# A GRU with a mixture of experts behind it: gates in three stages, and up projections without transposes of act

## The chip, the cores and the metric

The kernel runs on one core of a Trainium2 chip. The metric is the device time of one execution in microseconds (us). Beside it stand the profile of one execution and its trace, taken by the hardware profiler. The engines are named as in the profile: PE is TensorE (PEld its weight loads), DVE is VectorE, ACT is ScalarE, POOL is GpSimd, SP is SyncE.

## The reference, cut to what matters

`x` has 8 sequences of 256 steps with 512 features. A GRU runs over the steps, and its states go through a feed-forward block with one shared expert of 1024 inner features and eight routed experts of 256, two for each token. All is float32.

```
for each step:
    gi = x_t @ W_ih + b_ih                  # 512 -> 3 * 512
    gh = h @ W_hh + b_hh
    r = sigmoid(i_r + h_r);  z = sigmoid(i_z + h_z)
    n = tanh(i_n + r * h_n)
    h = (1 - z) * n + z * h
probs = softmax(h @ w_gate);  two experts per token, weights renormalised
routed = sum over the two: weight * ((silu(g) * u) @ w_down[e]),   g, u = split(h @ w_gate_up[e])
shared = (silu(g) * u) @ w_sh_down,                                g, u = split(h @ w_sh_gate_up)
out = x + routed + shared
```

## The kernel before, in words

**Recurrence.** `step(n)` (L348) is one of 256 steps. The batch is only 8, so the weights of a matmul are 8 columns of the transposed state `hT`, and W_hh is the moving operand. The 512 outputs of a gate are split into four column groups `j` that use four parts of TensorE's columns side by side, each writing its own 32 partitions of PSUM. Gates r and z share the tile `ps_rz` (256 columns), n has `ps_n` (128). ScalarE puts the seeds of the next step into PSUM ahead of the matmuls (`open_gates`, L337): the input part of r and z, and the bias of n. After the matmuls VectorE transposes `ps_rz` (L364) and `ps_n` (L370) in blocks of 32, ScalarE takes the sigmoid of r and z together (L366) and the tanh (L375), and VectorE makes the new state from `omz` = 1 - z, `zh` = z * h and `nn` (L379 to L383). GpSimd copies the state into `hc`, which collects the 16 states of a block of 128 tokens (L386).

A float32 matmul shows as two records in the trace, each with a weight load. A matmul in column groups is four such pairs, one for each group.

**Filler.** While the gates are being computed, TensorE works off a queue of pieces: the input projections of coming blocks (`project`, L282; tile `gip`), and the shared expert for the block of 16 steps that is complete. `MM` = 0.86 is the planner's cost of a piece, and pieces can be halved. After each step the main loop (L778) issues so many pieces that the queue of the block is spread evenly over the steps that are left. The instructions of an engine run in the order in which they are issued, so a step's matmuls stand behind the filler that was issued before them.

**Shared expert.** It is cut into four units of 256 inner features (`shared_unit`, L630, through `unit`, L570). A unit has four up pieces (one for each quarter `q` of the 512 features): the tokens are the weights, in four groups of 32 columns (`multiply`, L255), and 512 columns of `wsu` move past; tile `gu_s`. Then comes `gated` (L564): a sigmoid on ScalarE and two products on VectorE give `act`, with tokens on the partitions. `turn` (L586) transposes `act` with two 128x128 matmuls into `actTp_s`, and ScalarE copies that to `actT_s`. Two down pieces (tile `po`) then use `actT_s` as weights. `feed` (L709) interleaves the units: the first half of a unit's up pieces, the turn of the unit two feeds back, the second half, then the downs. A block's last unit is turned and finished in the next block.

**Other users of TensorE.** The transposes of `x` (`xTp`) and of `hc` (`hrp`, `send_rows` L486), and the router (`choose` L394, tile `lgp`; `order_experts`, `weigh`, `give_places`). PSUM has one buffer for `ps_rz`, one for `ps_n`, three for `ps_mm`, two for transposes (`ps_t`) and one for `po`.

**After the last step** `by_groups` is false: `multiply` then issues full 128-column matmuls. The last block's shared units run with the routing work between them (L806). Then 39 tiles of 128 token-expert pairs (`tile_unit`, L653) run: rows fetched by an indirect DMA on GpSimd's queue, transposed (`xrTp`), up (`gu_t`), turned (`actTp_t`), down (`yp`), and added into the output by an indirect DMA.

## Time and profile before

| | |
|---|---|
| device time, three runs | 1550.34, 1552.07, 1553.2 us; median 1552.07 us |
| the profiled execution | 1548.32 us, of which the span from first to last instruction is 1546.5 us |
| granted TensorE clock, mean of the span | 0.992 |
| busy | PE 1487.6, PEld 778.0, DVE 688.4, ACT 359.6, POOL 210.5 us |
| recurrent matmuls | ps_rz 8192 records, mean 380 ns; ps_n 8192 records, mean 273 ns |
| shared experts' up, gu_s | 257.0 us busy; records of 512 columns mean 594 ns, of 256 columns 380 ns |
| transposes of act in the shared experts, actTp_s | 128 records, 27.7 us busy, mean 298 ns |
| their copies on ScalarE, actT_s | 64, 23.5 us busy, mean 368 ns |
| seeds on ScalarE | ps_rz 256 copies, mean 369 ns; ps_n 256 copies, mean 259 ns |

How to read it: a row of a group gives the line, engine, operation, tiles and shapes, then busy time and the mean of one, then the idle time of the engine ahead of such instructions and what ended it. In `128*8 128x256` the part before the space is the weights (rows * columns), the part after it what moves past. Records of matmuls overlap: [...] In the timeline, a line begins with the start and the length in us of a merged group of instructions.

### The profile page before, as it was taken

Reading aid. Unit: us, or ns where it says so; the run is one execution under the profiler, and the core shown is the slowest. Engines: PE = TensorE matmul, PEld = TensorE weight load, DVE = VectorE, ACT = ScalarE, POOL = GpSimd, SP = SyncE. Lnnn points to the kernel's source line nnn. Section 1 sums busy time; section 2 is a strip of 40 time slices with the busy share of each in tenths; the row PEclk is TensorE's granted clock in tenths of the full one; section 3 lists DMA queues with packets and bytes.
Section 4 is the critical chain, followed back from the end, with each engine's and each line's share of the span. In section 5 each row is a group of like instructions: output and inputs, shape, how many; then the busy total and the mean of one; then the engine's idle time right before and its main releaser. Section 6 shows DMA issues by size and latency. Waiting matters only on the chain.

```text
span 1546.5 us, 53864 instructions
## 1 busy us (share of the span) xinstructions
PE 1487.6 (96%) x22969; PEld 778.0 (50%) x22969; DVE 688.4 (45%) x2747; ACT 359.6 (23%) x1351; POOL 210.5 (14%) x419
## 2 busy tenths in 40 slices
PE   4999999999999999999999999999999999999997
PEld 1455555555555555555555555555555544444443
DVE  2445454545454445454545454545454542222222
ACT  0222222222222222222222222222222221222221
POOL 2001110101000001010101010101010102444443
PEclk8999999999999999999999999999999999999998
DMA  7613130303020202010201010101010314445454
GB/s 256 201 40 108 14 87 13 100 13 101 13 60 13 60 13 59 14 52 15 57 16 50 17 41 18 48 18 48 18 53 13 84 49 135 75 89 96 84 93 62
DMA packets 59055, 92.70 MB, mean 60 GB/s; under 512 B 8960, under 2 KB 29504, under 8 KB 58816
## 3 DMA queue, kind: packets, MB, share of 16 engines
q1 hardware_dynamic: 48056, 66.89, 14.8%
q0 software_dynamic: 10624, 22.10, 7.7%
q8 instruction: 182, 2.98, 0.8%
q14 instruction: 57, 0.47, 0.1%
q10 hardware_dynamic: 136, 0.26, 0.1%
HBM read 57.85 MB, written 31.37 MB: 58 GB/s over the span
## 4 chain that ended last, share of the span: by engine, by line
PE 91%; DVE 4%; issue 2%; ACT 1%; DMA 1%; DVEq 0%; SPq 0%; POOLq 0%; POOL 0%; ACTq 0%
PE ps_rz L355 29%; PE ps_n L355 15%; PE gu_s L260 12%; PE gip L260 10%; PE gu_t L574 9%; PE po L260 6%; PE yp L679 4%; PE actTp_s L589 1%; DVE gn L370 1%; PE xrTp L660 1%; PE lgp L398 1%; ACT nn L375 1%; DMA x<-in_x_dram 1%; DVE nt L372 1%; DVE nt L373 1%
## 5 line engine op out<-in xcount | busy, mean ns | idle before, releaser
L355 PE MATMUL ps_rz<-we,hT 128*8 128x256 f32 x8192 | 491.2, 380 | 21.4 <-DVE hT L383 10.8
L355 PEld LDWEIGHTS ps_rz<-we,hT 128*8 128x8 f32 x8192 | 223.2, 89 | 298.8 <-ACT ps_n L343 56.3
L364 DVE STREAM_TRANSPOSE gT<-ps_rz 128x256 f32<-128x256 f32 x256 | 115.2, 450 | 397.2 <-PE ps_rz L355 397.1
L355 PE MATMUL ps_n<-we,hT 128*8 128x128 f32 x8192 | 271.9, 273 | 0.0
L260 PE MATMUL gu_s<-wsu,hc 128*32 128x512 f32 (+2 forms) x2376 | 257.0, 518 | 0.0
L355 PEld LDWEIGHTS ps_n<-we,hT 128*8 128x8 f32 x8192 | 225.9, 90 | 53.2 <-issue 0.5
L366 ACT ACTIVATE rz<-gT 128x64 f32<-128x64 f32 x256 | 65.6, 256 | 710.1 <-DVE gT L364 710.1
L386 POOL COPY hc<-hT 128x32 f32<-128x32 f32 x256 | 62.3, 243 | 1111.4 <-DVE hT L383 1111.4
L260 PE MATMUL gip<-we,xT 128*32 128x512 f32 (+1 forms) x1952 | 189.7, 510 | 2.1 <-ACT xT L247 2.1
L574 PE MATMUL gu_t<-we,xrT 128*128 x312 | 146.7, 593 | 0.2 <-ACT xrT L662 0.2
L260 PE MATMUL po<-wsd,actT_s 128*32 128x512 f32 (+2 forms) x1132 | 131.2, 532 | 13.3 <-ACT actT_s L591 13.3
L370 DVE STREAM_TRANSPOSE gn<-ps_n 128x128 f32<-128x128 f32 x256 | 81.1, 317 | 122.5 <-PE ps_n L355 115.2
L260 PEld LDWEIGHTS gu_s<-wsu,hc 128*32 128x32 f32 (+1 forms) x2376 | 77.2, 111 | 89.2 <-issue 79.4
L375 ACT ACTIVATE nn<-nt 128x32 f32<-128x32 f32 x256 | 58.7, 229 | 185.1 <-DVE nt L373 185.1
L341 ACT COPY ps_rz<-seeds 128x256 f32<-128x256 f32 x256 | 94.5, 369 | 22.0 <-DMA seeds<-gid_rz 21.5
L260 PEld LDWEIGHTS gip<-we,xT 128*32 128x32 f32 x1952 | 58.0, 110 | 72.2 <-issue 60.9
L567 DVE TENSOR_TENSOR act_t<-gu_t,act_t 128x256 f32<-128x256 f32 x39 | 16.6, 424 | 146.3 <-ACT act_t L566 146.3
L685 POOL DMA_INDIRECT out_dram<-y,row x39 | 61.6, 1579 | 124.7 <-DVE y L682 95.8
L679 PE MATMUL yp<-we,actT_t 128*128 x156 | 73.4, 593 | 0.5 <-ACT actT_t L591 0.5
L574 PEld LDWEIGHTS gu_t<-we,xrT 128*128 128x128 f32 x312 | 53.3, 190 | 38.7 <-issue 38.0
L260 PEld LDWEIGHTS po<-wsd,actT_s 128*32 128x32 f32 (+1 forms) x1132 | 38.0, 112 | 57.8 <-issue 33.5
L343 ACT COPY ps_n<-seed_hn 128x128 f32<-128x128 f32 x256 | 66.4, 259 | 0.0
(139 smaller groups left out, 974.1 us busy)
## 6 DMA issues: line engine op xcount, KB each, us to landing
gid_rz<-gi SPq DMA_DIRECT2D x16, 512.0 KB
seeds<-gid_rz SPq DMA_DIRECT2D x256, 32.0 KB
we<-in_L_ffn_w_gate_up_dram SPq DMA_DIRECT2D x8, 1024.0 KB
gid_n<-gi SPq DMA_DIRECT2D x16, 256.0 KB
seeds_n<-gid_n SPq DMA_DIRECT2D x256, 16.0 KB
wsu<-_L_ffn_w_sh_gate_up_dram SPq DMA_DIRECT2D x8, 512.0 KB
rows<-hr SPq DMA_DIRECT2D x16, 256.0 KB
again<-in_x_dram SPq DMA_DIRECT2D x16, 256.0 KB
```

Of the source, the lines that this page charges most:

```text
L260: nc.tensor.matmul(ps[rows_], lhs[:, rows_], rhs, start=start, stop=stop, skip_group_check=True)
L341: nc.scalar.copy(ps_rz, seeds[c % NS][:, t, 0 : 2 * P])
L343: nc.scalar.copy(ps_n, seed_hn)
L355: nc.tensor.matmul(ps[32 * j : 32 * j + B, :].rearrange("p (a i) -> p a i", i=32), hT[:, q, 0:B], whh_v[:, q, lo:hi, j, :], start=False, s ...
L364: nc.vector.transpose(gT.rearrange("p a b -> p (a b)"), ps_rz)
L366: nc.scalar.activation(rz, gT[:, :, 0:B], AF.Sigmoid)
L370: nc.vector.transpose(gn.rearrange("p a b -> p (a b)"), ps_n)
L375: nc.scalar.activation(nn, nt, AF.Tanh)
L386: nc.gpsimd.tensor_copy(hc_of[k].rearrange("p q (b t) -> p q b t", t=TS)[:, :, :, t], new)
L574: multiply(box["ps"][:, cols], lhs(q), w_up(q)[:, cols], start=(q == 0 and cols.start == 0), stop=(q == NQ - 1 and cols.stop == D),)
L679: nc.tensor.matmul(box["y"], lhs, rhs, start=(f == 0), stop=(f == NF - 1))
L685: nc.gpsimd.indirect_dma_start(out=out.rearrange("b t d -> (b t) d"), out_offset=bass.IndirectOffsetOnAxis(ap=laid["row"][:, i : i + 1], a ...
```

## The change

The diff, cut to its core:

```diff
-    ps_t = ctx.enter_context(tc.tile_pool(name="ps_t", bufs=2, space=PSUM))
+    ps_t = ctx.enter_context(tc.tile_pool(name="ps_t", bufs=1, space=PSUM))
...
+    banks = {g: ps_gru.tile([P, D], F32, name=f"ps_{g}") for g in "rnz"}
...
+    def for_transposes(shape, name):
+        if by_groups[0]:
+            return ps_t.tile([P, *shape], F32, tag="tp", name=name)
+        spare.rotate(-1)
...
     def step(n):
...
+        for g, bank in banks.items():
+            lo = "rzn".index(g) * NQ
             for q in range(NQ):
                 for j in range(4):
                     nc.tensor.matmul(
-                        ps[32 * j : 32 * j + B, :].rearrange("p (a i) -> p a i", i=32),
+                        bank[32 * j : 32 * j + B, 0:P].rearrange("p (a i) -> p a i", i=32),
                         hT[:, q, 0:B],
-                        whh_v[:, q, lo:hi, j, :],
+                        whh_v[:, q, lo : lo + NQ, j, :],
...
+        gr = turned("r")
+        r = made("r")
+        nc.scalar.activation(r, gr, AF.Sigmoid)
+        open_gate(n + 1, "r")
+        gn = turned("n")
+        nt = made("nt")
+        nc.vector.tensor_tensor(nt, gn, r, ALU.mult)
+        open_gate(n + 1, "n")
         nc.vector.tensor_tensor(nt, nT_of[c][:, ts, :, 0:B], nt, ALU.add)
+        nn = made("nn")
         nc.scalar.activation(nn, nt, AF.Tanh)
+        gz = turned("z")
+        z = made("z")
+        nc.scalar.activation(z, gz, AF.Sigmoid)
+        open_gate(n + 1, "z")
+        hn = made("hn")
+        nc.vector.tensor_tensor(hn, hT[:, :, 0:B], nn, ALU.subtract)
+        nc.vector.tensor_tensor(hn, z, hn, ALU.mult)
+        nc.vector.tensor_tensor(new, nn, hn, ALU.add)
...
     def shared_unit(k, c, n):
...
+            for q in qs:
+                for g in range(4):
+                    fs = slice(f * P + 32 * g, f * P + 32 * g + 32)
+                    nc.tensor.matmul(
+                        box["ps"][32 * g : 32 * g + 32, m, :],
+                        wsu[c][:, q, two_i, fs],
+                        hc_of[k][:, q, :],
...
+                    lambda cols, f=f: into(f, cols, box["act"][:, f, :], wsd[c][:, f, cols])
...
+    def feed_at_once(stages):
+        assert not stages[0] and under_way["up"] is None
+        under_way["up"] = stages
+        feed(None)
...
+    spare.extend(banks.values())
```

The gates get a PSUM bank each, `ps_r`, `ps_n` and `ps_z`, and TensorE computes them in this order. Each has its own seed copy, its own 32-block transpose on VectorE and its own activation. The new state is n + z * (h - n).

In a shared unit the roles of the operands are swapped for the up projections. 32 columns of `wsu` are the weights of each column group, the 128 tokens of `hc` move past, and `gu_s` and `act` have inner features on the partitions. One up piece is one of the four blocks of 128 inner features over all `q`. The down pieces use `act` as weights, and the unit has no turn. The up matmuls stay in column groups after the last step too. `feed_at_once` queues a unit's ups and then the downs of the unit before it; a block's last downs still go into the next block, behind its first unit's ups.

`ps_t` has one buffer. After the last step transposes take the three gate banks in turn. Expert tiles are computed as before.

More of the change, by code (lines that the diff above doesn't have):

```diff
@@ L229 @@
     nc.gpsimd.dma_start(listed[E * NM : E * NM + 1], vacant[0:1])
-    ps_rz = ps_gru.tile([P, 2 * P], F32, name="ps_rz")
-    ps_n = ps_gru.tile([P, P], F32, name="ps_n")
-    for ps in (ps_rz, ps_n):
-        n = ps.shape[-1]
-        nc.tensor.matmul(ps, seeds[0][:, 0, 0:P], seeds[0][:, 0, 0:n], start=True, stop=True)
-    xT_of = {}
+    banks = {g: ps_gru.tile([P, D], F32, name=f"ps_{g}") for g in "rnz"}
+    for bank in banks.values():
+        nc.tensor.matmul(
+            bank[:, 0:P], seeds[0][:, 0, 0:P], seeds[0][:, 0, 0:P], start=True, stop=True
+        )
+    xT_of = {}
+    by_groups = [True]
+    spare = deque()
+    def for_transposes(shape, name):
+        if by_groups[0]:
+            return ps_t.tile([P, *shape], F32, tag="tp", name=name)
+        spare.rotate(-1)
+        n = shape[0] * (shape[1] if len(shape) > 1 else 1)
+        bank = spare[0][:, 0:n]
+        return bank if len(shape) == 1 else bank.rearrange("p (a b) -> p a b", b=shape[1])
     def transpose_x(k):
-        ps = ps_t.tile([P, NQ, P], F32, tag="tp", name=f"xTp_{k}")
+        ps = for_transposes([NQ, P], f"xTp_{k}")
         for q in range(NQ):
@@ L251, in transpose_x @@
             load_x(k + 2)
-    by_groups = [True]
     def multiply(ps, lhs, rhs, start, stop):
@@ L335, with open_gate @@
     nT_of = {}
-    def open_gates(n, part):
+    def open_gate(n, g):
+        if n >= T:
+            return
         c, t = divmod(n, SC)
-        if part == 0:
-            nc.scalar.copy(ps_rz, seeds[c % NS][:, t, 0 : 2 * P])
-        else:
-            nc.scalar.copy(ps_n, seed_hn)
+        src = {"r": seeds[c % NS][:, t, 0:P], "z": seeds[c % NS][:, t, P : 2 * P], "n": seed_hn}
+        nc.scalar.copy(banks[g][:, 0:P], src[g])
     whh_v = whh.rearrange("p q (a j i) -> p q a j i", j=4, i=32)
@@ L351, in step @@
         hT, new = states[n % NH], states[(n + 1) % NH][:, :, 0:B]
-        for ps, lo, hi in ((ps_rz, 0, 2 * NQ), (ps_n, 2 * NQ, 3 * NQ)):
+        for g, bank in banks.items():
+            lo = "rzn".index(g) * NQ
             for q in range(NQ):
@@ L362, in step, with turned, made @@
                     )
-        gT = state.tile([P, 2 * NQ, 32], F32, tag="gT", name=f"gT_{n}")
-        nc.vector.transpose(gT.rearrange("p a b -> p (a b)"), ps_rz)
-        rz = state.tile([P, 2 * NQ, B], F32, tag="rz", name=f"rz_{n}")
-        nc.scalar.activation(rz, gT[:, :, 0:B], AF.Sigmoid)
-        if n + 1 < T:
-            open_gates(n + 1, 0)
-        gn = state.tile([P, NQ, 32], F32, tag="gn", name=f"gn_{n}")
-        nc.vector.transpose(gn.rearrange("p a b -> p (a b)"), ps_n)
-        nt = state.tile([P, NQ, B], F32, tag="nt", name=f"nt_{n}")
-        nc.vector.tensor_tensor(nt, gn[:, :, 0:B], rz[:, 0:NQ, :], ALU.mult)
+        def turned(g):
+            gT = state.tile([P, NQ, 32], F32, tag=f"{g}T", name=f"{g}T_{n}")
+            nc.vector.transpose(gT.rearrange("p a b -> p (a b)"), banks[g][:, 0:P])
+            return gT[:, :, 0:B]
+        def made(name):
+            return state.tile([P, NQ, B], F32, tag=name, name=f"{name}_{n}")
+        gr = turned("r")
[6 more added lines that the diff above has]
+        open_gate(n + 1, "n")
         nc.vector.tensor_tensor(nt, nT_of[c][:, ts, :, 0:B], nt, ALU.add)
-        nn = state.tile([P, NQ, B], F32, tag="nn", name=f"nn_{n}")
+        nn = made("nn")
         nc.scalar.activation(nn, nt, AF.Tanh)
-        if n + 1 < T:
-            open_gates(n + 1, 1)
-        omz = state.tile([P, NQ, B], F32, tag="omz", name=f"omz_{n}")
-        nc.vector.tensor_scalar(omz, rz[:, NQ:, :], -1.0, 1.0, ALU.mult, ALU.add)
-        zh = state.tile([P, NQ, B], F32, tag="zh", name=f"zh_{n}")
-        nc.vector.tensor_tensor(zh, rz[:, NQ:, :], hT[:, :, 0:B], ALU.mult)
-        nc.vector.tensor_tensor(nn, omz, nn, ALU.mult)
-        nc.vector.tensor_tensor(new, nn, zh, ALU.add)
+        gz = turned("z")
[6 more added lines that the diff above has]
+        nc.vector.tensor_tensor(new, nn, hn, ALU.add)
         if t == 0:
@@ L488, in send_rows @@
         hc = hc_of[k]
-        ps = ps_t.tile([P, D], F32, tag="tp", name=f"hrp_{k}")
+        ps = for_transposes([D], f"hrp_{k}")
         for q in range(NQ):
@@ L551, in lay_tiles @@
         else:
-            ps = ps_t.tile([P, 2, P], F32, tag="tp", name="listp")
+            ps = for_transposes([2, P], "listp")
             for v in range(2):
@@ L568, in gated, with unit @@
         nc.vector.tensor_tensor(act, ps[:, IM : 2 * IM], act, ALU.mult)
-    def unit(name, box, lhs, w_up, w_down_, done, before_=None, multiply=nc.tensor.matmul):
+    def unit(name, box, lhs, w_up, w_down_, done, before_):
         def up(q, cols):
@@ L573, in up @@
                 box["ps"] = ps_mm.tile([P, 2 * IM], F32, tag="mm", name=f"gu_{name}")
-            multiply(
-                box["ps"][:, cols],
-                lhs(q),
-                w_up(q)[:, cols],
-                start=(q == 0 and cols.start == 0),
-                stop=(q == NQ - 1 and cols.stop == D),
+            nc.tensor.matmul(
+                box["ps"], lhs(q), w_up(q), start=(q == 0), stop=(q == NQ - 1)
             )
@@ L586, in turn @@
         def turn():
-            ps = ps_t.tile([P, NF, P], F32, tag="tp", name=f"actTp_{name}")
+            ps = for_transposes([NF, P], f"actTp_{name}")
             for f in range(NF):
@@ L630, in shared_unit, with up, up_piece @@
     def shared_unit(k, c, n):
-        return unit(
-            f"s{c}_{k}",
-            {},
-            lambda q: hc_of[k][:, q, :],
-            lambda q: wsu[c][:, q].rearrange("p two f -> p (two f)"),
-            lambda f: wsd[c][:, f, :],
-            into_block(k, c, n),
-            multiply=multiply,
+        box = {}
+        def up(m, qs):
+            if m == 0 and qs[0] == 0:
+                box["ps"] = ps_mm.tile([P, 2 * NF, P], F32, tag="mm", name=f"gu_s{c}_{k}")
+            two_i, f = divmod(m, NF)
+            for q in qs:
+                for g in range(4):
+                    fs = slice(f * P + 32 * g, f * P + 32 * g + 32)
+                    nc.tensor.matmul(
+                        box["ps"][32 * g : 32 * g + 32, m, :],
+                        wsu[c][:, q, two_i, fs],
+                        hc_of[k][:, q, :],
+                        start=(m == 0 and q == 0),
+                        stop=(q == NQ - 1),
+                        skip_group_check=True,
+                    )
+            if m == 2 * NF - 1 and qs[-1] == NQ - 1:
+                box["act"] = three.tile([P, NF, P], F32, tag="act", name=f"act_s{c}_{k}")
+                gated(box["ps"].rearrange("p m t -> p (m t)"), box["act"].rearrange("p f t -> p (f t)"))
+        def up_piece(m):
+            half = NQ // 2
+            parts = (range(half), range(half, NQ))
+            return (
+                MM,
+                lambda: up(m, range(NQ)),
+                [(MM / 2, lambda qs=qs: up(m, qs)) for qs in parts],
+            )
+        into = into_block(k, c, n)
+        return (
+            [],
+            [up_piece(m) for m in range(2 * NF)],
+            [],
+            [
+                matmul_piece(
+                    lambda cols, f=f: into(f, cols, box["act"][:, f, :], wsd[c][:, f, cols])
+                )
+                for f in range(NF)
+            ],
         )
@@ L656, in before_ @@
         def before_():
-            ps = ps_t.tile([P, NQ, P], F32, tag="tp", name=f"xrTp_{i}")
+            ps = for_transposes([NQ, P], f"xrTp_{i}")
             xr = xr_of.pop(i)
@@ L713, in feed @@
         ups = last[1] if last else []
-        queue.extend(stages[0] if stages else [])
+        if ups:
+            queue.extend(stages[0] if stages else [])
         queue.extend(ups[: NQ // 2])
@@ L718, in feed @@
         queue.extend(oldest[3] if oldest else [])
+        if not ups:
+            queue.extend(stages[0] if stages else [])
         under_way.update(up=stages, turn=last)
+    def feed_at_once(stages):
+        assert not stages[0] and under_way["up"] is None
+        under_way["up"] = stages
+        feed(None)
     def fill():
@@ L734 @@
             turn_seeds(0)
-    for part_no in range(2):
-        open_gates(0, part_no)
+    for g in banks:
+        open_gate(0, g)
     load_shared()
@@ L774 @@
         if k > 0:
-            for u in [*(shared_unit(k - 1, c, NSH) for c in range(NSH)), None]:
-                feed(u)
+            for c in range(NSH):
+                feed_at_once(shared_unit(k - 1, c, NSH))
         over = 0.0
@@ L812 @@
     ]
-    for u in [*(shared_unit(k, c, NSH) for c in range(NSH)), None, None]:
-        feed(u)
+    for c in range(NSH):
+        feed_at_once(shared_unit(k, c, NSH))
     spent = 0.0
```

## The prediction

> **What bounds the kernel now.** I read the page's engine rows and chain first, then the windows by stage, then the timeline of single steps.

> ```profile
> PE 1487.6 (96%) x22969; PEld 778.0 (50%) x22969; DVE 688.4 (45%) x2747; ACT 359.6 (23%) x1351; POOL 210.5 (14%) x419
> ...
> PE 91%; DVE 4%; issue 2%; ACT 1%; DMA 1%; DVEq 0%; SPq 0%; POOLq 0%; POOL 0%; ACTq 0%
> ```

> TensorE holds 91% of the chain; no other engine is busy half the time. So a change is worth what it takes from TensorE's row of work, plus the holes in it. Where are the holes?

> ```profile
> 420.00:740.00 320.00, 315.80 (x5736) 169.09 (x5732) 157.70 (x665) 78.40 (x318) 23.74 (x74) 1.00 0.13 35
> ...
> 1274.00:1309.50 35.50, 31.35 (x115) 14.79 (x104) 11.80 (x51) 5.38 (x17) 6.42 (x8) 0.90 0.39 130
> 1309.50:1546.50 237.00, 226.24 (x694) 110.04 (x694) 62.37 (x117) 51.70 (x116) 96.88 (x75) 0.98 0.47 85
> ```

> Three stages: 256 recurrent steps (35.7 to 1274 us), a handover (35.5 us, clock only 0.90), 39 expert tiles (237 us). A matmul row lasts some 0.17 us longer than the time until the next round can start, so "busy" hides holes. I therefore took starts, as in these steps on TensorE:

> ```profile
> 617.58 1.90 PE L260 MATMUL gu_s<-wsu,hc 128*32 128x512 f32 x16
> 619.67 1.91 PE L355 MATMUL ps_rz<-we,hT 128*8 128x256 f32 x32 [0.19 <-DVE hT L383]
> 621.39 1.06 PE L355 MATMUL ps_n<-we,hT 128*8 128x128 f32 x32
> 622.26 1.91 PE L260 MATMUL gu_s<-wsu,hc 128*32 128x512 f32 x16
> 624.10 0.44 PE L589 MATMUL actTp_s<-ident,act_s 128*128 128x128 f32 x2
> 624.47 0.83 PE L355 MATMUL ps_rz<-we,hT 128*8 128x256 f32 x12
> ```

> Four column groups run side by side, so 32 rows are 8 rounds. From start to next start: ps_n takes 0.873 us (621.39 to 622.26) (109 ns a round of 128 columns), ps_rz 1.727 us (216 ns a round of 256), gu_s 1.72 us for four rounds of 512 where nothing waits (429 ns). What exceeds this is lost: 617.58 to 619.67 is 2.09, so 0.37 waited for hT; 622.26 to 624.10 is 1.84, so 0.12 went into leaving the 32-column form. Summed so over the steps: waits of ps_rz for hT cost 25.4 us; the 59 pairs of act transposes there cost 33.6 us by their own starts (14 of them, at a block's head where the down projection follows at once, wait 0.94 us each for ScalarE's copy, 13.1 us in all) and 6.8 us in the work ahead of them: 40.4 us.

> The wait for hT is this chain:

> ```profile
> 606.10 1.06 PE L355 MATMUL ps_n<-we,hT 128*8 128x128 f32 x32
> ...
> 607.29 0.32 DVE L370 STREAM_TRANSPOSE gn<-ps_n 128x128 f32<-128x128 f32 x1 [0.49 <-PE ps_n L355]
> ...
> 607.72 0.19 DVE L372 TENSOR_TENSOR nt<-gn,rz 128x32 f32<-128x32 f32 x1
> 607.94 0.19 DVE L373 TENSOR_TENSOR nt<-nT,nt 128x32 f32<-128x32 f32 x1
> ...
> 608.17 0.23 ACT L375 ACTIVATE nn<-nt 128x32 f32<-128x32 f32 x1 [0.74 <-DVE nt L373]
> ...
> 608.43 0.19 DVE L382 TENSOR_TENSOR nn<-omz,nn 128x32 f32<-128x32 f32 x1
> ...
> 608.73 0.19 DVE L383 TENSOR_TENSOR hT<-nn,zh 128x32 f32<-128x32 f32 x1
> ```

> The last ps_n matmul starts at 606.89, hT ends at 608.92: 2.03 us. The next ps_rz starts at best 0.145 us after hT (the least over all steps), so 2.17 us from the last start, of which the last round uses 0.11: filler of under 2.06 us leaves TensorE waiting. Four half pieces are 1.72, five 2.15.

> **The change, part by part.**
> Transposes of act in the steps: gone, with their mode changes and the copy's wait: -40.4 us. The down projection now reads act itself; in the order of the changed kernel a unit's down follows four up pieces later (3.5 us), against 0.38 + 0.42 + 0.42 us of gating, so no new wait. The 64 copies to actT (0.37 us) leave ScalarE, which is no bound.

> Recurrent matmuls: r, n, z are 24 rounds of 109 ns, 2.62 us, for 2.60: +0.02 x 256 = +5 us.

> Up projections: a unit was 8 rounds of 512 (3.43 us) and is 32 rounds of 128, with 32-column weights. No row before has weights of 32 columns at 128 wide. Nearest is ps_n, 109 ns, with 8 columns (load row 90 ns against 110). Low end: 107 ns, half of a 512's quarter, 429/4. High end: the load grows with its row, +20 ns, say 131. I take 109: the x transposes load 128 columns (141 ns a row) and still follow each other by 109 ns, so a load longer than the round is hidden. 32 x 0.109 = 3.50: +0.066 x 60 units = +4 us (at 131 ns, +44 over all 64).
> [...] In the trace ps_n's loads start 2 ns after the previous matmul of their group, and the round stays 109 ns. I go by the row.

> Gates: the chain now ends in z. From z's last matmul start, by the rows above: 0.40 to the transpose (as for gn), 0.32 for it, 0.10 to ScalarE (gT's end 606.80 to rz 606.90), 0.23 sigmoid (as tanh, 128x32), 0.03 back, 0.29 from the product's start to the last op's, 0.19 for it: 1.56, and 0.145: 1.71 us for 2.17. The n branch must be ready: n ends 0.87 before z; tanh ends 1.51 after n's last start, 0.64 after z's; h - n follows z's transpose on VectorE at about 0.73 and is done before z's sigmoid (1.05). Filler needed: 1.60 us. I counted the filler between steps in the changed kernel's order on TensorE: 11 steps (in the last block, without projections) have 1.2 to 1.3 us, 99 have about 1.72, the rest 2.1 or more. So waits are 11 x 0.3 = 3.6 us: 3.6 - 25.4 = -21.8. The cover is thin: four halves exceed the need by 0.12 us. Bounds: at 1.95 us the shortfall of all steps is 18 us, at 2.17 (nothing won) 43; below 1.6 at most 2 more are won.
> VectorE's step stays: 3 x 0.317 + 5 x 0.192 for 0.450 + 0.317 + six of about 0.19, 1.9 us each. ScalarE's seeds are 3 x 0.26 for 0.37 + 0.26; with three 0.23 activations 1.47 us in a step of 4.6. The z seed is queued behind the sigmoid of z and before filler's ScalarE work, which only meets the next r, ready 0.5 us early. With that cover gone a gating at the filler's end would cost up to 0.5 us in its step; I take 0.
> One bank for x and hr transposes instead of two: 32 uses, the next mostly steps away, one pair in the same step; 0 to 1 us, taken as 0. DMAs, SP's and POOL's orders hold; block outputs leave four up pieces later, which only the 'again' buffers meet.

> Handover: before, TensorE idles 2.69 us at 1277.6 since actT's copy stands behind two router sigmoids in ScalarE's queue, then runs at half rate (granted clock 0.50 in 1280 to 1284). [...] the row shows it after 2.69 following 0.74 and a few tiny matmuls. [...] by the row 2.7 and some 2.9 of slow rounds (6.40 us from 1280.29 to 1286.69 for 8 matmuls that take 3.44). Afterwards up rounds follow the router at once. New sum: 1.8 to the router, 0.9, ups 14.0, downs 5 x 1.72, transposes 0.7, twelve mode changes of 0.12 in and 0.15 out, as around the act transposes, 1.6, small ones 0.3, first tile 1.3: 29.2; I add 0.5 for row fetches (3.6 us to landing, 4.9 us of work over them): 29.7 for 35.5: -5.8.
> Tiles: 12 x 0.429 + 6 x 0.109 = 5.80 against 5.81 us from tile to tile: at its floor and untouched. Three banks for two: 0.

> Sum: -40.4 + 5 + 4 - 21.8 - 5.8 = -59 us. The profiled execution has a span of 1546.5 (1548.3 in all), hence 1487.5; the median shown, 1552.07, lies 3.75 above that execution, hence 1493.

> **The rivals.**
> *The wait returns.* The chain isn't shortened as added up: handovers between engines happen three times a step, and gated ops stand on VectorE ahead of r. For it: 99 steps have only 0.12 us to spare. Against: all terms are rows. At 1.95 us +14.6: 1508; at 2.17 +39.6: 1533. Chance 0.17.
> *Weight loads set the up round, mildly.* At 131 ns +44, less some waits: 1535. For it: 110 ns loads in 109 ns rounds. Against: the x transposes. 0.09.
> *Weight loads do not overlap.* One mechanism, at the up rounds, that makes the kernel slower: 59 us over 2048 rounds is 29 ns, so from 138 ns a round on it loses; [...] against it ps_n. 0.05.
> *The change does less than it says:* the planner spreads the saved time so that the pieces wait elsewhere. For it: halves of 0.43 us are coarse. Against: the counted order. It would leave the 40 us of transposes, about 1512; in the first rival's chance.

> **How the numbers follow.** My main case, 1481 to 1505 around 1493, has 0.65; still faster, below 1481, 0.04; the rivals 0.17, 0.09, 0.05. The range runs from 1478 to 1532, leaving out the slower rival, most of the mild one and the lowest tail. A measurement can tell about 0.2% from no change: faster 0.94, same 0.01, slower 0.05.

> **What would show it.** No transposes of act_s; up rounds 109 ns apart; 1.56 us from z's last matmul start to hT; ps_r waiting for hT in few steps outside the last block; the recurrence ending some 53 us earlier, the clock at 1.00 after it, tiles at 5.81 us. Wrong if up rounds pass 115 ns, or if most four-half steps wait.

## The result, and the profile after

The changed kernel takes 1540.99 us (median of 13 runs, 1535.48 to 1549.62), the kernel before 1551.13 (13 runs, 1548.91 to 1553.2): a ratio of 0.9937 [0.9919, 0.9954]. That is a gain of 10 us where 59 were forecast. The profiled execution of the changed kernel is one of its fastest, 1535.54 us with a span of 1533.8. Its runs spread over 14 us, those of the kernel before over 4.

First the page: TensorE's row, the instruction queue, the chain, and the groups of the up matmuls and their weight loads.

```profile
PE 1472.5 (96%) x36779; PEld 1155.0 (75%) x36779; DVE 731.0 (48%) x2747; ACT 435.5 (28%) x1799; POOL 210.2 (14%) x419
...
q8 instruction: 290, 4.75, 1.3%
...
PE 95%; issue 2%; DMA 1%; ACT 0%; SPq 0%; DVE 0%; POOLq 0%; POOL 0%; DVEq 0%; ACTq 0%
...
L659 PE MATMUL gu_s<-hc,wsu 128*32 128x128 f32 x8192 | 281.0, 274 | 8.3 <-issue 7.9
L659 PEld LDWEIGHTS gu_s<-hc,wsu 128*32 128x32 f32 x8192 | 253.0, 110 | 30.1 <-issue 20.9
```

The chain gave up its 4% of VectorE, as the prediction wanted. But TensorE has 13,810 more records, and the queue that brings instructions by DMA has 108 more packets. Its row before, which the prediction did not look at:

```profile
q8 instruction: 182, 2.98, 0.8%
```

The columns are packets, MB and share. In the trace each packet of this queue has 16,384 bytes; a record is a matmul and its weight load, counted here as two instructions. 108 more packets for 2 x 13,810 = 27,620 more instructions are 255.7 a packet. I take 256, which makes 64 bytes each: an estimate from these counts. With it 290 packets are 74,240 instructions, against 2 x 36,779 = 73,558, and before 46,592 against 45,938. The counts agree to 1.4%, so I take this queue to be the one that brings TensorE its instructions.

The windows by stage, with TensorE's busy time in the third column:

```profile
114.00:190.00 76.00, 65.34 (x1855) 53.91 (x1851) 35.00 (x138) 19.33 (x86) 11.39 (x22) 0.98 0.26 62
190.00:420.00 230.00, 224.23 (x6643) 192.16 (x6637) 120.52 (x477) 70.27 (x310) 17.28 (x53) 1.00 0.21 56
420.00:740.00 320.00, 318.35 (x9495) 272.55 (x9489) 171.34 (x678) 100.62 (x444) 24.08 (x75) 1.00 0.14 37
...
1264.00:1296.00 32.00, 29.69 (x586) 20.54 (x577) 11.63 (x50) 3.65 (x12) 6.44 (x8) 1.00 0.45 146
1296.00:1533.80 237.80, 226.24 (x694) 110.00 (x694) 62.36 (x117) 51.55 (x116) 96.83 (x75) 0.98 0.48 84
```

In the middle TensorE is busier than before (318.35 for 315.80), the handover took 32.0 us for 35.5 at a full clock, the tiles are as they were. The first row stands out: from 114 to 190 us TensorE has over 10 us of nothing. The same window of the kernel before:

```profile
114.00:190.00 76.00, 74.98 (x1383) 40.77 (x1383) 37.76 (x161) 18.14 (x75) 11.92 (x24) 1.00 0.25 61
```

What TensorE waited for in the changed kernel (total us, times, longest):

```profile
PE gu_s L659 <- issue: 7.9, 7, 3.3
PE ps_r L368 <- issue: 7.3, 6, 1.9
PE ps_z L368 <- issue: 4.9, 8, 2.1
PE ps_n L368 <- issue: 2.3, 4, 1.0
```

No row of `hT` is left (the account below still finds 2.6 us). Instead there are waits that nothing in the profile released ("issue"); among TensorE's waits in the kernel before there is no such row. Two of them on TensorE's timeline:

```profile
156.62 1.06 PE L659 MATMUL gu_s<-hc,wsu 128*32 128x128 f32 x32
161.03 1.29 PE L659 MATMUL gu_s<-hc,wsu 128*32 128x128 f32 x20 [3.35 <-issue]
...
233.81 0.86 PE L659 MATMUL gu_s<-hc,wsu 128*32 128x128 f32 x22
236.47 1.80 PE L659 MATMUL gu_s<-hc,wsu 128*32 128x128 f32 x57 [1.80 <-issue]
```

The same matmuls, with operands that have long been there, stop in the middle of a piece and go on. I compared the end of each such hole with the packets of the instruction queue:

| last start before the hole (us) | lost (us) | fetch began | fetch took (us) | fetch's end to next matmul (us) |
|---|---|---|---|---|
| 53.68 | 1.71 | 53.01 | 1.05 | 1.44 |
| 157.41 | 3.51 | 158.50 | 1.12 | 1.42 |
| 180.51 | 1.81 | 179.55 | 1.34 | 1.53 |
| 186.68 | 2.05 | 184.94 | 2.51 | 1.38 |
| 234.40 | 1.96 | 233.93 | 1.23 | 1.31 |
| 1227.01 | 2.29 | 1227.19 | 0.94 | 1.28 |

Of 50 holes over 0.15 us in the recurrence (31.5 us), 26 (24.9 us), all over 1 us among them, end 1.25 to 1.7 us after a fetch has ended, and three small ones 1.2 us after. The other 21 (5.9 us) are of a second kind: each begins 0.8 to 1.2 us after GpSimd starts a scatter of router entries, with no fetch that ended 1.2 to 1.7 us before. Why TensorE stops there is not shown. In the kernel before, with the same scatters, there are 7 holes (1.5 us), all in its first step, where the granted clock is still 0.50. Its fetches take as long as those of the changed kernel (1.05 us in the median, 2.5 at most); TensorE does not stop after any of them.

The long holes of the changed kernel lie where other DMAs are in flight (298 GB/s in all from 233.0 to 234.5 us, ahead of the hole after 234.40): beside the loads at the start (53.68 us), at the eight scatters of router entries (145 to 187 us, one a step) and at the expert loads (one a block from 190 to 420 us, more at 1200 to 1231).

At the longest hole the clock is lower, too. From 160.4 to 163.8 us, as it ends and after, the granted clock is 0.50, and the 12 up rounds (48 records) that begin from 161.03 on take 209 ns each in the mean instead of 109. In the account that follows, such loss stands under holes and slips.

An account of the recurrence, from its first to its last gate matmul, follows from the starts of all TensorE records. The floor is each round at its own length (109, 216 or 429 ns, and 60 or 110 ns for the small ones). Form changes are what is lost between matmuls in column groups and full ones, with the waits for copies that fall there (and, in the changed kernel, e9 and e12, a stop of 1.7 to 1.8 us around 150 us, ahead of a gate, which also ended 1.3 to 1.4 us after a fetch). Holes are all other losses of over 40 ns beyond the usual distance to the next record, slips the rest.

| us | recurrence | floor | waits for hT | form changes | holes | slips |
|---|---|---|---|---|---|---|
| before | 1238.3 | 1161.5 | 24.9 | 33.5 | 6.8 | 11.6 |
| after | 1228.4 | 1157.5 | 2.6 | 12.2 | 36.2 | 20.0 |

So 47.6 us were gained in the floor, the waits and the form changes, and 37.8 given back: 29.4 in holes and 8.4 in slips.

### The profile page after: what moved, and what is told of

Same layout as the page of the kernel before. It is cut to its first block, busy times and chain, and to the rows that moved or that the text cites. A ratio compares the mean times of both kernels' runs of the same rounds, so it can differ in the third digit from the quotient of the medians.

```text
span 1533.8 us, 82162 instructions
## 1 busy us (share of the span) xinstructions
PE 1472.5 (96%) x36779; PEld 1155.0 (75%) x36779; DVE 731.0 (48%) x2747; ACT 435.5 (28%) x1799; POOL 210.2 (14%) x419
## 3 DMA queue, kind: packets, MB, share of 16 engines
q1 hardware_dynamic: 48056, 66.89, 15.1%
## 4 chain that ended last, share of the span: by engine, by line
PE 95%; issue 2%; DMA 1%; ACT 0%; SPq 0%; DVE 0%; POOLq 0%; POOL 0%; DVEq 0%; ACTq 0%
PE ps_r L368 15%; PE gu_s L659 15%; PE ps_n L368 15%; PE ps_z L368 15%; PE gip L272 11%; PE gu_t L595 9%; PE po L272 7%; PE yp L731 4%; PE lgp L419 1%; DMA x<-in_x_dram 1%; PE xTp L259 1%; PE hrp L512 1%; PE ps_r L712 0%; PE ps_z L712 0%; PE ps_n L712 0%
## 5 line engine op out<-in xcount | busy, mean ns | idle before, releaser
L368 PE MATMUL ps_r<-we,hT 128*8 128x128 f32 x8192 | 294.8, 273 | 17.6 <-ACT ps_r L355 9.5
L368 PE MATMUL ps_z<-we,hT 128*8 128x128 f32 x8192 | 299.2, 273 | 5.6 <-issue 4.9
L368 PEld LDWEIGHTS ps_r<-we,hT 128*8 128x8 f32 x8192 | 240.4, 90 | 76.9 <-issue 32.8
L659 PE MATMUL gu_s<-hc,wsu 128*32 128x128 f32 x8192 | 281.0, 274 | 8.3 <-issue 7.9
L659 PEld LDWEIGHTS gu_s<-hc,wsu 128*32 128x32 f32 x8192 | 253.0, 110 | 30.1 <-issue 20.9
L368 PEld LDWEIGHTS ps_z<-we,hT 128*8 128x8 f32 x8192 | 242.2, 90 | 13.2 <-issue 11.5
L379 DVE STREAM_TRANSPOSE rT<-ps_r 128x128 f32<-128x128 f32 x256 | 80.8, 316 | 272.0 <-PE ps_r L368 271.1
L379 DVE STREAM_TRANSPOSE nT<-ps_n 128x128 f32<-128x128 f32 x256 | 81.1, 317 | 144.4 <-PE ps_n L368 144.2
L272 PE MATMUL po<-wsd,act_s 128*32 128x512 f32 (+2 forms) x1108 | 138.8, 537 | 1.4 <-issue 1.4
L355 ACT COPY ps_n<-seed_hn 128x128 f32<-128x128 f32 x256 | 69.0, 269 | 104.1 <-DVE nT L379 103.0
L379 DVE STREAM_TRANSPOSE zT<-ps_z 128x128 f32<-128x128 f32 x256 | 81.0, 316 | 18.1 <-PE ps_z L368 9.8
```

The source lines that it names most:

```text
L272: nc.tensor.matmul(ps[rows_], lhs[:, rows_], rhs, start=start, stop=stop, skip_group_check=True)
L355: nc.scalar.copy(banks[g][:, 0:P], src[g])
L368: nc.tensor.matmul(bank[32 * j : 32 * j + B, 0:P].rearrange("p (a i) -> p a i", i=32), hT[:, q, 0:B], whh_v[:, q, lo : lo + NQ, j, :], sta ...
L379: nc.vector.transpose(gT.rearrange("p a b -> p (a b)"), banks[g][:, 0:P])
L659: nc.tensor.matmul(box["ps"][32 * g : 32 * g + 32, m, :], wsu[c][:, q, two_i, fs], hc_of[k][:, q, :], start=(m == 0 and q == 0), stop=(q = ...
```

## The experiments

The theory, *instruction supply*: TensorE's time also depends on how many instructions it must be brought. A round of 128 columns in four groups is 8 instructions in 109 ns, so a packet of 256 would last 3.5 us; a round of 256 columns takes twice as long (216 ns) over as many, 7 us a packet (both estimates from the rows). When a fetch is late beside other DMAs, TensorE would run dry. Rivals: the loss sits in the new up rounds (their loads of 32 columns), or TensorE stops for a reason of its own, whatever the DMAs do.

**One part at a time.** Only the gates (e1: the changed kernel with the up projections of before), only the up projections (e2: the kernel before with the changed ones), and the kernel before with one edit (e3): its matmuls of 256 columns for r and z cut into two of 128, all else kept.

```diff
e1, to the changed kernel:
-                    nc.tensor.matmul(box["ps"][32 * g : 32 * g + 32, m, :], wsu[c][:, q, two_i, fs], hc_of[k][:, q, :],
+            multiply(box["ps"][:, cols], lhs(q), w_up(q)[:, cols],
...
e2, to the kernel before:
-            lambda q: hc_of[k][:, q, :],
-            lambda q: wsu[c][:, q].rearrange("p two f -> p (two f)"),
+                        wsu[c][:, q, two_i, fs],
+                        hc_of[k][:, q, :],
...
e3, to the kernel before:
-        for ps, lo, hi in ((ps_rz, 0, 2 * NQ), (ps_n, 2 * NQ, 3 * NQ)):
+        for ps, at_, lo in ((ps_rz, 0, 0), (ps_rz, P, NQ), (ps_n, 0, 2 * NQ)):
...
-                        whh_v[:, q, lo:hi, j, :],
+                        whh_v[:, q, lo : lo + NQ, j, :],
```

e1: 

> The three gate stages alone, shared experts as before (act is transposed, up rounds of 512 columns). Theory 'instruction supply': TensorE's stream of 64-byte instructions runs dry, so the loss follows the number of TensorE instructions. By the rows the gates save 20 us (waits for hT 25 to 3 us, recurrent matmuls +5 us): 1531 us; 8192 of the 13810 added records come with the gates, so they bring 8192/13810 of the missing 37 us of the recurrence, +22: about 1550, with holes put down to 'issue' in the middle of runs of matmuls. Rival 'up rounds': the holes come from rounds of 128 columns with weight loads of 32 columns; there are none here, so 1531 and no such holes.

e2: 

> The up projections by inner dimension alone, gates as before. By the rows: transposes of act -40 us, up rounds +4, waits for hT +15 (filler shorter, chain of 2.17 us), handover -4: about 1526 us. Instruction supply: 5600 more records, +15: about 1541. Rival 'up rounds': all of the 37 us: about 1563, slower than before.

e3: 

> The kernel before, with each matmul into ps_rz (256 columns) made as two of 128 columns into the same tile: the same sums in the same order of stages, 8192 more records with their loads, nothing else. By the rows +5 us: 1556. Instruction supply: +22 more: about 1578, with holes put down to 'issue' where expert weights are loaded. Rival 'up rounds': 1556 and no new holes.

Measured: e1 1546.05 us, 0.9971 [0.9958, 0.9985]; e2 1538.33, 0.9925 [0.9912, 0.9939]; e3 1575.21, 1.0166 [1.0153, 1.0179]. The theory had forecast about 1550, 1541 and 1578 us. e3 is the sharpest. Its floor rises by the forecast 5.3 us, its waits for hT and form changes stay (24.2 and 33.5), and the recurrence is 28.2 us longer (25 in the median), with 14.9 us more of holes and 8.7 of slips. Its page and TensorE's waits:

```profile
PE 1504.8 (96%) x31161; PEld 1004.5 (64%) x31161; DVE 689.3 (44%) x2747; ACT 359.6 (23%) x1351; POOL 210.8 (13%) x419
...
q8 instruction: 246, 4.03, 1.1%
```

```profile
PE ps_rz L355 <- DVE hT L383: 10.3, 41, 0.7
...
PE ps_rz L355 <- issue: 6.0, 15, 2.2
...
PE ps_n L355 <- issue: 2.0, 3, 1.4
```

Besides the number of instructions only the width of the gate matmuls changed, and `ps_n`'s of that width had no such waits in the kernel before; now the waits on `issue` came. No up round was touched, so the loss does not need them, against the first rival. But not all of it is shown to be late fetches: of 14 us in e3's holes over 0.15 us, 7 us follow a fetch and 7 us stand at scatters, and the slips are not located. e2 alone gains as much as the whole change, within the intervals: its holes rise only to 13.8 us (226 fetches), but without the transposes as filler its waits for hT rise to 39.7 us.

**Other DMAs out of the way.** e4 takes the expert loads out of the recurrence. e5 cuts them into pieces over twice the blocks (128 KB each, by the profile's DMA issues, where a whole load of up weights is 1024 KB). e6 spreads the eight scatters as well, one a block. e7 is the up projections alone (e2) with e6's spreads and up pieces that can be quartered. In e6 and e7 entries of the first block's list overwrite some of later blocks', so that some routed rows differ, for the same work. e8 is the changed kernel once more, beside e5 to e7.

```diff
e4:
-        if 1 <= k <= E - 4:
+        if k == NB:
...
e5:
-            when(6, 0, lambda k=k: load_expert(k - 1))
+            for i in range(6):
+                when(2 + 2 * i, 0, lambda k=k, i=i: load_piece((k - 1) // 2, ((k - 1) % 2) * 6 + i))
...
e6, besides:
-            for i in range(2 if k > 1 else E):
+            if k <= E:
+                when(4 if k == 1 else 2, 0, lambda k=k: enter(0, k - 1))
...
e7, besides, on e2:
+                    (MM / 2, lambda qs=qs: up(m, qs), [(MM / 4, lambda q=q: up(m, [q])) for q in qs])
```

e4: 

> The changed kernel without the six expert loads (9 MB) that run during the recurrence; tiles of experts 0 to 3 use expert 4's weights, 6 and 7 use what lies in their place, so the routed part of the output is another one and the work is the same. Instruction supply, delayed by bulk transfers on the same DMA engines: the holes in the windows 114 to 420 us and after 1190 us go, some 20 to 25 us: about 1518. If the supply is short whatever else the DMA engines do, or by the rival 'up rounds': 1541 as the changed kernel.

e5: 

> The changed kernel with the expert loads of the recurrence cut into pieces of 256 KB: experts 0 to 3 one piece every second step over eight blocks, 6 and 7 two pieces a step in the last block. The same bytes, in bursts of 0.7 us instead of 4.2 us (256 KB and 1.5 MB at the 360 GB/s of the handover). Instruction supply, with bursts as what delays a fetch: most of the 16 us that the kernel without these loads gained, about 1529. If it is the bytes that count: 1541.

e6: 

> The same, and the eight scatters of the first block's router entries, which go out one a step in steps 4 to 11 of the second block, go out one a block over eight blocks. Without the loads, holes of 0.5 to 1.8 us still stood some 5 us apart from 151 to 183 us, in those steps. If the scatters delay fetches there: 6 to 8 us less than with spread loads alone, about 1522. If the holes there come from the dense up rounds that begin at that place: no difference to spread loads alone, 1529.

e7: 

> The up projections by inner dimension alone, with gates as before, up pieces that the planner can also cut in quarters, and both spreads. Instruction supply: the stream is shorter here (226 fetches for 290), holes were 14 us in the profile and fall to about 5; quarters even out filler and save some 3 us of waits for hT: 1538 - 12, about 1526. If holes don't come from the supply: 1535.

e8: 

> The changed kernel itself on the same chip as the three above, so that they are compared with it directly: 1541 by either theory, with holes at the same places (145 to 187 us, once a block in 190 to 420 us, around 1200 to 1231 us).

Measured: e4 1525.41 us, 0.9843 [0.9827, 0.9858]; e5 1535.27, 0.9889 [0.9872, 0.9907]; e6 1524.24, 0.9833 [0.9814, 0.9852]; e7 1527.37, 0.9844 [0.9831, 0.9856]; e8 1542.37, 0.9941 [0.9929, 0.9954]. Where the holes went is seen by window. In e4, without loads:

```profile
114.00:190.00 76.00, 68.45 (x1986) 56.37 (x1982) 35.62 (x144) 20.18 (x91) 11.35 (x22) 1.00 0.19 42
190.00:420.00 230.00, 228.90 (x6830) 198.28 (x6825) 124.43 (x490) 72.17 (x319) 17.54 (x54) 1.00 0.14 36
```

and in e6, which spreads the scatters:

```profile
114.00:190.00 76.00, 75.44 (x2275) 64.16 (x2271) 42.17 (x163) 23.54 (x105) 5.20 (x18) 1.00 0.19 53
```

From 190 to 420 us TensorE's busy time rises from 224.23 us in the changed kernel to 228.90 without the loads; from 114 to 190 only the spreading of the scatters brings it back, 65.34 to 75.44. The second rival falls: what the DMAs do decides where TensorE stops. e5 gained 7 us on e8, half of what was expected, and its profiled execution has as many holes as e8's (37.1 and 38.5 us): from 190 to 420 us TensorE's busy time is 228.81 us, as without loads, but from 420 to 740, where the later pieces now go, it falls from 318.35 to 314.69. Cutting the loads alone moves holes more than it removes them.

**Both ways of spreading with the list whole, and a shorter stream.** e9 writes the first block's list within two blocks (six scatters in the first, two in the next, two steps apart), with e5's loads. e11 is the same on e7. e10 is e9 with the shorter stream: r and n in one matmul of 256 columns, then z. e12 is that without any spreading.

```diff
e9:
-            for i in range(2 if k > 1 else E):
+            for i in {1: range(6), 2: range(6, E)}.get(k, ()):
+                when(4 + 2 * i if k == 1 else 2 * (i - 6), 0, lambda i=i: enter(0, i))
e10 (on e9) and e12 (on the changed kernel):
-        for g, bank in banks.items():
+        for g, v in (("rn", whh_rn), ("z", whh_z)):
...
-        gr = turned("r")
+        grn = turned("rn", 2)
+        gr, gn = grn[:, 0:NQ, :], grn[:, NQ:, :]
```

e9: 

> The changed kernel with the expert loads in pieces of 256 KB, and the first block's eight scatters one every second step (steps 4 to 14 of the second block, 0 and 2 of the third) instead of one every step; output as the reference. Instruction supply, delayed by scatters: holes of 7 us at 145 to 190 us shrink, about 1527, between 1535 (loads in pieces alone) and 1524 (one scatter a block). If a scatter costs its hole wherever it stands: 1535.

e11: 

> The up projections alone, gates as before, pieces of up work down to quarters, loads and scatters spread as in the two others; output as the reference. 1527 was measured with one scatter a block; about 1529 here by instruction supply.

e10: 

> The same, with the gates in two stages: r and n in one matmul of 256 columns, then z of 128. This takes 8192 records (a third of the recurrence's) from TensorE's stream, the work stays (2.60 us a step). By the rows of before the chain from z's last matmul start to hT becomes 1.93 us (r's sigmoid can't start before n is done), so the filler needed is 1.97 us for 1.60, and waits for hT rise from 3 to about 33 us. Instruction supply: holes fall to the 5 us of the shorter streams; together about 1523 to 1530. If holes don't follow the number of instructions: 1527 + 30 = 1557.

e12: 

> r and n of a step in one matmul of 256 columns as in e10, but with the loads and list entries where the changed kernel has them. TensorE's recurrent stream has 16 rounds a step instead of 24, so about as many instructions as with the up projections changed alone (226 fetches). Instruction supply: the holes are those of that kernel, some 14 us, instead of 36, so with e10's other terms about 1505. If mainly the moved loads made e10 fast, not the shorter stream: 1515 to 1525.

Measured: e9 1524.61 us, 0.984 [0.9826, 0.9853]; e11 1523.34, 0.9837 [0.9823, 0.985]; e10 1494.85, 0.9659 [0.9646, 0.9672]; e12 1505.4, 0.9727 [0.9713, 0.974]. e12 came out at the 1505 that the theory said. That it did so to within half a microsecond is luck: its five runs spread over 6 us, and the forecast started from e10's measured time and added the 10 us by which holes should differ (in the account they differ by 7). The accounts of the profiled executions:

| us | fetches | recurrence | floor | waits for hT | form changes | holes | slips |
|---|---|---|---|---|---|---|---|
| e1, gates alone | 246 | 1238.1 | 1166.8 | 2.0 | 29.8 | 20.7 | 18.8 |
| e2, ups alone | 226 | 1232.8 | 1152.1 | 39.7 | 10.6 | 13.8 | 16.6 |
| e3, before, split | 246 | 1266.5 | 1166.8 | 24.2 | 33.5 | 21.7 | 20.3 |
| e9, after, spread | 289 | 1218.3 | 1157.5 | 2.1 | 11.9 | 31.7 | 15.1 |
| e11, ups, spread | 226 | 1215.6 | 1152.1 | 34.9 | 11.1 | 4.6 | 12.9 |
| e12, r and n in one | 226 | 1194.1 | 1152.1 | 6.6 | 12.1 | 10.8 | 12.5 |
| e10, that, spread | 225 | 1185.0 | 1152.1 | 6.4 | 10.6 | 3.9 | 12.0 |

From the changed kernel to e12 the recurrence is 34.3 us shorter: 25.4 in holes, 7.5 in slips, 5.4 in the floor, and 4.0 more in waits. Some 6 us of the holes are of the second kind, of which e9 to e12 have none over 0.15 us; these four ran on two other chips than e1 to e8, so whether the kernels or the chips did that stays open. Spreading then takes 0.7% (e10), on the long stream 1.0% (e9 against e8), in the direction of the theory; with these intervals the difference is not shown, nor that a late fetch costs less where a packet lasts longer.

e9's profiled execution is 19 us shorter than e8's, and only 7 us of that are holes. The clock is part of the rest: in e8 it is 0.50 for 17.0 us of the recurrence after the start, in four places, each behind a hole of 2.5 to 3.8 us, in e9 for 3.4 us. If a round took about twice as long there, as measured above (209 ns for 109), the difference is worth up to 6.8 us (an estimate).

The clearest pair is e9 and e10, the same loads and scatters on the same chip, with the long and the short stream: holes fall from 31.7 to 3.9 us. In the window from 420 to 740 us TensorE is busy for 313.04 us in e9. e10's page, the same window, and its waits:

```profile
PE 1452.7 (97%) x28587; PEld 922.6 (62%) x28587; DVE 664.9 (45%) x2491; ACT 431.3 (29%) x1799; POOL 210.2 (14%) x419
...
q8 instruction: 225, 3.69, 1.1%
```

```profile
420.00:740.00 320.00, 319.79 (x7398) 214.52 (x7394) 158.26 (x631) 100.69 (x452) 26.22 (x78) 1.00 0.20 51
```

```profile
PE ps_rn L376 <- DVE hT L414: 2.7, 10, 0.3
...
PE ps_rn L376 <- issue: 0.2, 1, 0.2
```

The 25 `issue` waits of the four rows of the changed kernel are down to one of 0.2 us in the gates and none in the up matmuls; one of 1.2 us is left in the down projections. I had expected 1523 to 1530 of e10, with 33 us of waits for hT, since z's transpose would stand behind r's and n's. In the trace it and z's sigmoid run under the n branch, and from z's last start to `hT` it is 1.71 us, not 1.93. e10 beats both kernels. e11, with the gates of before (and up pieces that can be quartered), is as fast as e9: the three gate stages gained nothing even with the DMAs spread.

## Why the prediction was wrong, point by point

**The step that failed** is the way the prediction summed TensorE's rounds in "Recurrent matmuls: r, n, z are 24 rounds of 109 ns, 2.62 us, for 2.60: +0.02 x 256 = +5 us", and likewise for the ups. The rounds do take that long, but a term was missing, and so put at nothing: what the added instructions cost beyond their rounds. By e3 the split of the recurrent matmuls costs 25 us where 5 were summed. In the whole change it is 29.4 us of holes, and with them go 8.4 us of slips. Most of the time in the holes over 0.15 us (24.9 of 31.5 us) ends 1.25 to 1.7 us after a fetch; the part at scatters and the slips are not explained. The count was to be seen: the page has the row of the instruction queue, and the change takes 256 recurrent steps from 16 rounds to 24 and 64 units from 8 rounds to 32. The cost was not: the kernel before stops after none of its fetches.

**The other terms**, in the account of the profiled executions:

- *Transposes, gates and ups*, -40.4 + 5 + 4 = -31.4 forecast. Measured: floor -4.0, form changes -21.3, together -25.3. No transpose of `act_s` is left, up rounds follow each other by 109 ns, a step's gates by 0.873 us. The transposes account for about 34 of the 40.4 us (12.9 of floor, 118 of 109 ns each, and 21.3 of form changes); where the prediction counted the other 6 too many was not found.
- *Waits for hT*, 25.4 to 3.6 forecast: 24.9 to 2.6. The chain was forecast at 1.56 us from z's last start to `hT`, and is 1.49 (median; 2.03 before). One step of the changed kernel, where z's last round starts 0.11 us ahead of the next matmul, at 601.22:

```profile
600.46 1.06 PE L368 MATMUL ps_z<-we,hT 128*8 128x128 f32 x32
...
601.33 1.47 PE L272 MATMUL gip<-we,xT 128*32 128x256 f32 x16
...
601.58 0.32 DVE L379 STREAM_TRANSPOSE zT<-ps_z 128x128 f32<-128x128 f32 x1
...
601.99 0.23 ACT L398 ACTIVATE z<-zT 128x32 f32<-128x32 f32 x1
...
602.25 0.19 DVE L403 TENSOR_TENSOR hn<-z,hn 128x32 f32<-128x32 f32 x1 [0.17 <-ACT z L398]
602.55 0.19 DVE L404 TENSOR_TENSOR hT<-nn,hn 128x32 f32<-128x32 f32 x1
```

- *Handover*, -5.8 forecast: 35.5 to 32.0, -3.5. The long idle time and the slow clock behind it are gone (1.00 for 0.90); two stops on `issue`, 0.34 and 1.07 us, are new. *Tiles*: 237.8 us for 237.0.
- *Sum*: -25.3 - 22.3 + 29.4 + 8.4 - 3.5 + 0.8 = -12.5, against the 12.7 us from a span of 1546.5 to one of 1533.8. The median gained 10: this execution of the changed kernel lies 5.5 us below its median, that of the kernel before 2.8 below its own.

**The rivals.** None of them was it. The wait for hT did not return. The up round is 109 ns (in the line at 156.62, 8 rounds last 1.06 us, of which 0.27 is the last record) with loads of 110 ns; so loads that do not overlap, which would make it 219 ns (109 + 110), did not come, nor did 131 ns. The planner did not spread the saved time away: the waits and the form changes went down. The loss went where no rival pointed, which is why the range missed too. The prediction gave no chance to a cost of the larger number of matmuls beyond their rounds.

**What stays open.** The slips (each 40 ns or less) rise with the number of instructions, 11.6 to 20.0 us, and e3 shows the same 8.7, but they are not located. Neither is it shown how the holes at scatters arise. Why a fetch begins late beside scatters and loads is not in the profile: some begin only after TensorE has stopped (158.50 for the hole at 157.41). How far ahead a fetch is asked for was not measured.

## What to carry to other kernels

Count a change's instructions as well as its rounds: packets in the instruction queue's row times 256, against the time in which TensorE uses them up. Here three gate rounds of 3.5 us a packet beside other DMAs lost 36 us of holes, where r and n at 7 us a packet lost 11 (packet times estimated from the rows). Here the wider moving operand was the better one: r and n in one matmul of 256 columns took 0.9727 of the kernel before (e12), in two of 128 columns 0.9937. Where the stream must be dense, try spreading loads and scatters; here that gave 1.0% (e9 against e8), while cutting the loads into pieces alone (e5) kept the holes, 37.1 us for 38.5. A wait on "issue" in the middle of a group of like matmuls was the sign to look for: 7 of them, 7.9 us, in the up matmuls of the changed kernel, none in those of the kernel before.
